# The end of a graph-attention layer issued together with the start of a top-p layer: shared banks and buffers, two hand-written first periods, graph parts loaded two ahead

## The chip, the cores and the metric

The kernel runs on one core of a Trainium2 chip. The metric is the device time of one execution in microseconds (us). Before the change three runs took 2077.24, 2079.14 and 2081.67 us; the median is 2079.14. The engines are named as in the profile: PE (matmul) and PEld (its weight loads), DVE (vector), ACT (scalar), POOL, and SP, whose queue (SPq) issues most transfers.

## What is computed

Two layers over N = 3327 nodes with 256 features and a dense 0/1 adjacency matrix. Both normalize and rectify their input and add their result to it.

```python
# layer 0: graph attention, 4 heads of 64
h = relu(layernorm(x))
support = (h @ weight) per head;  f1, f2 = support . weight_u, support . weight_v
attn = softmax over neighbours of leaky_relu(f1[m] + f2[n], 0.2)
x = x + attn @ support + bias + h @ proj_w.T + proj_b
# layer 1
h = relu(layernorm(x)); Xf = Xa = h; Z = 0
R = (adj + I) / row sums
for n in range(2):
    q = Xa @ W1.T @ W2.T;  k = Xa @ W3.T
    p = softmax(q @ k.T)
    A = p, only the largest entries of each row up to a sum of 0.9, normalized
    Xf = R @ Xf;  Xa = A @ Xa
    Z = Z + Xf @ U1[n].T + Xa @ U2[n].T
x = x + layernorm(h + Z) * ln_g + ln_b
```

## The kernel before

Rows are cut into NT = 26 tiles of 128 nodes (the last has 127).

**Layer 0** runs over four blocks of target nodes (tiles 0 to 5, 6 to 13, 14 to 21, 22 to 25). In each it goes over all 26 source tiles: a piece of the transposed adjacency is loaded (`load_adj`, L614), DVE makes one weight tile `w` per head (`weigh`, L581), and PE adds features and weight sums into PSUM (`sum_features` L590, `sum_weights` L601). POOL writes the adjacency back to DRAM as `adj_r` for layer 1. When a block is done, its sums are copied to `ot` (L675), and each of its row tiles passes through the class `Out` (L433): `divide` (transposes on PE), `normalize` (DVE, with three small POOL operations), `relu` (ACT, into `res`), `turn` (transposes on PE and a copy to `hT` on ACT), `keys` (the product with `wqk` on PE; `hi_and_lo` splits it in a high part on ACT and a low part on DVE), `take_keys` (two transfers into `k_sb`), `graph` (the product with `ug` on PE, two copies on ACT), `take_graph` (DVE), and stores on SP. For the first three blocks these steps are spread over the next block's steps. For the last block there is no next block: they stand alone, in L700 to L720, one row tile behind the other.

**Layer 1** runs two steps (s = 0 and 1). A step is a sequence of periods n. In each, a written list of words, a plan (`PLANS`, L1200), sets the order of work; each word names a role (`m2`, `m`, `a`, `b`, `c`, `d`: tile n+2, n+1, n, n-1, n-2, n-3) and a method of `Rows` (L798). A tile passes through

- `logits` 0 to 6 (L819): seven pieces of q times keys on PE. Piece 6 also needs the mean of all keys, which `mean_of_keys` puts behind the last key; `evict` (L831) copies a piece to `lg` by DVE (`v`) or ACT (`s`);
- `exp` (L839, ACT) and `guess` (L853, POOL): a first guess of where to cut the row;
- four times `probe` (L902): a pass of ACT over the row, which sums its exponentials behind the present guess; `go_on`, `aim` and `narrow` (ACT, DVE) make the next guess;
- `threshold`, `low` (L961), `largest` (L968), `last_kept`, `keep` (L1009): the exact cut, mostly on DVE;
- `transpose`, `copy_transposed`, `product` (L1019 to L1049): the kept row times the node features `xa`, on PE;
- small products and stores.

Beside this, R @ Xf is computed by `graph` (L737): per row tile seven parts of up to four chunks, each with a 256 KB load of `adj_r` (L748, three buffers `adjt`) and eight matmuls (L769, L770). The word `graph` in a plan issues the parts that are due: `PARTS` (L1283) gives the number for the first periods, and the rest of the 182 parts of a step are spread evenly over the other periods. `ends.dve` and `ends.act` finish a row of it (`add`, `high`, `low`).

The order on PE, DVE, ACT and POOL is the order of issue in the program (`in_traced_order`, L127); it isn't set for SP. Periods -3, -2 and -1 of step 0 hold the first words for tiles 0 and 1, after all of layer 0; the first plan serves n < 2. Layer 0's buffers (`p0`, `pa`, and the banks `ps1`) are given back before layer 1's (`px`, `pw`, `ps2`) are made; `lng`, `lnb` (L724) and `u_sb` (L1298) are loaded between them.

Of the kernel before, what the change touches and what calls it, by code (L numbers as in the profile page):

```python
# [10 lines left out]
FP = mybir.dt.float32  # L11
# [10 lines left out]
P = 128  # L22
# [32 lines left out]
def kernel(  # L55
# [189 lines left out]

    def part_of_keys(s, part):
        n = (EARLY if s else BLOCKS[-1][0] - 2) * P
        return ((0, n), (n, N))[part]
# [17 lines left out]
    def mean_of_keys(keys, s, part):  # L266

        k_sb, mean = keys
        n0, n1 = part_of_keys(s, part)
        nc.vector.tensor_reduce(  # L270
            mean[:, part : part + 1], k_sb[:, n0:n1].bitcast(FP), AX.X, ALU.add
        )
        if part == 1:
            nc.vector.tensor_scalar(
                k_sb[:, N:], mean[:, :1], mean[:, 1:], 1.0 / N, ALU.add, ALU.mult
            )

    EARLY = NT - 2

    def load_u(pool):  # L280
        u_sb = pool.tile([P, DC, 2, D], FP, name="u_sb")
        for n in range(STEPS):
            nc.sync.dma_start(out=u_sb[:, :, n, :], in_=u2t[n].rearrange("(c p) j -> p c j", p=P))
        return u_sb
# [23 lines left out]
    keys = new_keys(right)  # L308
    first_traced = len(nc.cur_bb.bb.instructions)
    with ExitStack() as l0:  # L310
        p0 = l0.enter_context(tc.tile_pool(name="p0", bufs=1))
        pa = l0.enter_context(tc.tile_pool(name="pa", bufs=2))
        ps = l0.enter_context(tc.tile_pool(name="ps1", bufs=1, space=PSUM))

        def bank(k, shape):
            return ps.tile(shape, FP, tag=f"b{k}", name="pt")

# [31 lines left out]
        sup = p0.tile([P, NT, D], FP, name="sup")  # L349
# [22 lines left out]
        def normalize(i):  # L372
            normed[i] = hn = pa.tile([P, D], FP, tag="x1", name="hn")
# [4 lines left out]
        def turn(i, k):  # L378
# [6 lines left out]
            hT = pa.tile([P, DC, P], FP, tag="hT", name="hT", bufs=4)  # L385
# [3 lines left out]
        def features(i, k):  # L389
# [9 lines left out]
            if i == t0:  # L399
                made["ef"] = pa.tile([H, 4, P], FP, tag="ef", name="ef", bufs=1)  # L400
            nc.scalar.activation(eas[:, i], f1, AF.Exp, scale=SLOPE)
            nc.scalar.activation(cf[:, i], f1, AF.Exp, scale=1.0 - SLOPE)
            nc.scalar.activation(made["ef"][:, i - t0], f2, AF.Exp, scale=SLOPE - 1.0)
            if i == t1 - 1:
                spread(t0, t1, made["ef"])
# [26 lines left out]

        class Out:  # L433
# [10 lines left out]
            def normalize(r):  # L444
# [5 lines left out]
                x1 = pa.tile([P, D], FP, tag="x1", name="x1")  # L450
# [33 lines left out]
            def turn(r, k):  # L484
# [6 lines left out]
                r.hT = pa.tile([P, DC, P], FP, tag="hT", name="hT", bufs=4)  # L491
# [56 lines left out]
        HP = H // 2  # L548
# [5 lines left out]
        for c in range(DC):  # L554
            for v, row in enumerate((u_row, v_row)):
                t = pa.tile([P, D], FP, tag="x1", name="wx")
# [14 lines left out]
        w1n = p0.tile([DA, DC, P], FP, name="w1n")  # L571
# [9 lines left out]
        def weigh(j, at, b, cn, *heads):  # L581
            pj = rows(j)
            for h in heads:
                ws[h] = w = pa.tile([P, CH], FP, tag="w", name="w", bufs=7)
# [29 lines left out]
        def load_adj(b, j):  # L614
            c0, pj = BLOCKS[b][0] * P, rows(j)
            cn = min(BLOCKS[b][1] * P, N) - c0
            ats[b, j] = at = pa.tile([P, CH], FP, tag="at", name="at", bufs=4)
# [11 lines left out]
        for step, (b, j) in enumerate(order):  # L629
# [41 lines left out]
            ot = pa.tile([P, HP + 1, CH], FP, tag="ot", name="ot", bufs=1)  # L671
# [28 lines left out]
        mean_of_keys(keys, 0, 0)  # L700
        n = len(outs)
        free = [3, 4, 5, 6, 7, 0, 1, 2]
        for k, r in enumerate(outs):
            r.divide(free[k])
        for k in range(n + 2):
            if k < n:
                outs[k].normalize()
            if 0 <= k - 2:
                outs[k - 2].keys(free[k - 2])
            if k < n:  # L710
                outs[k].relu()
            if 0 <= k - 2:
                outs[k - 2].take_keys()
            if 0 <= k - 1 < n:
                outs[k - 1].turn(free[n + k - 1])
        for k, r in enumerate(outs):
            r.graph(free[n + k])
            r.take_graph()
            r.store_keys()
            r.store()  # L720


    pl = ctx.enter_context(tc.tile_pool(name="pl", bufs=1))
    lng = row_of(pl, ln_g, "lng")  # L724
    lnb = row_of(pl, ln_b, "lnb")

# [10 lines left out]
    def graph(i, s, xf, ends):  # L737
# [5 lines left out]
        for g in range(NG):  # L743
            c0 = 4 * g
            a = pw.tile([P, 4, P], FR, tag="adjt", name="adjt", bufs=ADJ)
            cn = min(4, NT - c0)
            nf = min(cn, NF - c0)
            nc.sync.dma_start(  # L748
                out=a[:, :nf, :pn].bitcast(FP),
                in_=adj_r[c0 * P : (c0 + nf) * P, n0 : n0 + pn].rearrange("(c p) n -> p c n", p=P),  # L750
            )
            if nf < cn:
                move_rows(
                    nc.sync, a[:, nf, :pn].bitcast(FP), adj_r[NF * P :, n0 : n0 + pn], rows(NF)
                )
            if g == 3:
                while ends:
                    ends.pop(0)[1]()
                ad = pw.tile([P, D], FP, tag="ad", name="ad", bufs=1)
# [38 lines left out]
    class Rows:  # L798
# [32 lines left out]
        def evict(r, copy, *pieces):  # L831
            for p in pieces:
                if p == 0:
                    r.lg = pw.tile([P, N + 1], FP, tag="lg", name="lg", bufs=3)
# [4 lines left out]
        def exp(r):  # L839
# [8 lines left out]
            r.e = pw.tile([P, N], FP, tag="e", name="e", bufs=3)  # L848
# [53 lines left out]
        def probe(r):  # L902
# [3 lines left out]
            junk = pw.tile([P, N], F8, tag="junk", name="junk", bufs=1)  # L906
# [123 lines left out]
        def copy_transposed(r, copy, *groups):  # L1030
            for g in groups:
                pt = r.pt.pop(g)
                r.wt[g] = wt = pw.tile([P, 4, P], FP, tag="wt", name="wt", bufs=WT)
# [82 lines left out]
    def general_cut(i, s, k_sb, pows):  # L1116
# [42 lines left out]
        for m in range(MANT):  # L1159
# [42 lines left out]
            """  # L1202
            c.product.4 c.query ends.dve a.probe ends.dve m.logits.3 b.threshold m.logits.4
            c.product.3 ends.act m.evict.v.2 m.evict.s.4 m.evict.v.3 m.logits.5
            c.copy_transposed.v.5 a.go_on d.store_sum a.aim.1 d.high m.logits.6 c.product.5
            graph b.low a.probe c.transpose.1 graph m.evict.v.6 c.transpose.4
            c.copy_transposed.s.4 d.small_products c.product.2 m.evict.v.5 m.exp a.narrow.1
            m2.logits.0 graph c.transpose.2 c.product.0 a.aim.2 c.product.6 graph graph
            b.largest m2.logits.1 c.scale c.copy_transposed.v.2 a.probe d.store_features
            m2.evict.s.0 b.last_kept m2.logits.2 c.transpose.6 c.transpose.3 graph a.narrow.2  # L1210
            d.low_part b.keep c.copy_transposed.v.3 c.product.1 c.copy_transposed.v.0
            m2.evict.v.1 c.copy_features_t m.guess c.features_t a.aim.3 m3.queries a.probe
            c.transpose.0 a.narrow.3 c.copy_transposed.s.1 b.make_sure c.copy_transposed.v.6
            graph c.transpose.5
            """,
# [66 lines left out]

    PARTS = (  # L1283
        {-3: 0, -2: 0, -1: 3, 0: 7, 1: 8},
# [10 lines left out]
    with ExitStack() as fast:  # L1295
        ps = fast.enter_context(tc.tile_pool(name="ps2", bufs=2, space=PSUM))
        px = fast.enter_context(tc.tile_pool(name="px", bufs=1))
        u_sb = load_u(px)  # L1298
        pw = fast.enter_context(tc.tile_pool(name="pw", bufs=2))
# [9 lines left out]
        def parts_of_graph(s, xf):  # L1309
            for i in range(NT):  # L1310
                yield from graph(i, s, xf, graph_ends)
# [37 lines left out]

        for s in range(STEPS):  # L1350
            end = s == STEPS - 1
            plans = [[t.split(".") for t in p.split()] for p in PLANS[s]]
            for n in range(-3, NT + 3):
                plan = plans[0 if n < 2 else 1 if n < NT else 2]
                fills = sum(t == ["graph"] for t in plan)
                if s and n == -3:
                    continue
# [43 lines left out]
    with ExitStack() as gen:  # L1401
        ps = gen.enter_context(tc.tile_pool(name="ps3", bufs=2, space=PSUM))
# [101 lines left out]
```

## Time and profile before

| | us |
|---|---|
| median of three runs | 2079.14 |
| the profiled execution | 2080.33 |
| its span, first to last instruction | 2078.5 |
| layer 0 (to the last attention matmul) | 0 to 655.9 |
| from there to the first transpose of node tile 0 | 655.9 to 738.0 |
| steady periods of step s=0 | 25.98 each |
| steady periods of step s=1 | 23.8 to 24.0 each |

The span is shorter than the execution's own time by 1.8 us, which lie around it. Times below are us from the span's start. [...] The column of waits names what came last before an engine went on.

### The profile page before, as it was taken

The numbers are of one execution on the slowest core, as the hardware profiler recorded it, in microseconds if no ns is written. First come the engines' busy times: TensorE is split into PE (matmuls) and PEld (weight loads), VectorE is DVE, ScalarE is ACT, GpSimd is POOL, SyncE is SP. The second block draws the span as 40 slices with busy tenths as digits, with TensorE's granted clock in tenths as the row PEclk, the third lists the DMA queues.
The fourth block names the chain that finished last, engine by engine and source line by source line (L and its number), as shares of the span: only waits on it lengthen the run. The fifth ranks groups of instructions, "written<-read, shape, count | busy, mean of one in ns | idle before, by whom it ended". The sixth has DMA issues, their size and how long they took to land.

```text
span 2078.5 us, 34250 instructions
## 1 busy us (share of the span) xinstructions
PE 1988.8 (96%) x11474; PEld 1391.1 (67%) x11474; DVE 1710.0 (82%) x4055; ACT 1271.3 (61%) x1950; POOL 790.6 (38%) x1860
## 2 busy tenths in 40 slices
PE   7999999999998689999999999997999999999996
PEld 3343333233223578888888888876798898888885
DVE  5767888988886488888888888855899999999985
ACT  2110100101112788888888888838899999999982
POOL 3221231223332244444444444423554445544441
PEclk9999999999998899999999999999899999999998
DMA  5455556565564433333333333377244343344320
GB/s 180 140 163 175 196 191 226 168 217 191 171 190 138 136 86 101 102 96 99 103 98 103 102 100 103 102 220 206 64 105 117 104 108 95 101 106 111 99 74 20
DMA packets 318881, 270.60 MB, mean 130 GB/s; under 512 B 30200, under 2 KB 293879, under 8 KB 318568
## 3 DMA queue, kind: packets, MB, share of 16 engines
q1 hardware_dynamic: 304024, 216.04, 37.7%
q0 software_dynamic: 13504, 51.62, 7.0%
q8 instruction: 92, 1.51, 0.3%
q14 instruction: 93, 0.76, 0.1%
q10 hardware_dynamic: 1168, 0.67, 0.1%
HBM read 177.79 MB, written 88.62 MB: 128 GB/s over the span
## 4 chain that ended last, share of the span: by engine, by line
PE 49%; ACT 12%; DVE 3%; issue 2%; DMA 1%; POOL 0%; SPq 0%; ACTq 0%; DVEq 0%; POOLq 0%
PE acca L1046 23%; ACT junk L907 7%; PE pt L1025 6%; PE pg L826 6%; PE accr L769 5%; PE accr L770 5%; ACT e L849 2%; PE pz L1089 2%; DMA adjt<-adj_r 1%; ACT lg L837 1%; ACT aim L897 1%; DVE v L973 1%; ACT wt L1035 1%; PE pq L195 0%; PE pt L524 0%
## 5 line engine op out<-in xcount | busy, mean ns | idle before, releaser
L907 ACT ACTIVATE junk<-lg,at 128x3327 fp8e4<-128x3327 f32 (+1 forms) x208 | 637.8, 3067 | 13.0 <-POOL at L873 10.6
L588 DVE SCALAR_TENSOR_TENSOR w<-xf,cf,at 128x1024 f32<-128x1024 f32 (+4 forms) x416 | 425.6, 1078 | 52.3 <-PE pt L606 51.7
L769 PE MATMUL accr<-xf,adjt 128*128 128x258 f32 (+3 forms) x1352 | 367.8, 305 | 19.1 <-DMA adjt<-adj_r 15.3
L770 PE MATMUL accr<-xf,adjt 128*128 128x256 f32 (+1 forms) x1352 | 341.9, 285 | 0.0
L596 PE MATMUL pt<-w,sup 128*64 128x512 f32 (+5 forms) x1456 | 337.5, 576 | 1.1 <-DVE w L588 1.0
L1046 PE MATMUL acca<-xa,wt 128*128 128x256 f32 (+2 forms) x1352 | 317.9, 384 | 2.9 <-ACT wt L1035 2.9
L1046 PE MATMUL acca<-res,wt 128*128 128x256 f32 (+2 forms) x1352 | 317.8, 380 | 0.0
L769 PEld LDWEIGHTS accr<-xf,adjt 128*128 128x128 f32 (+1 forms) x1352 | 260.0, 192 | 29.5 <-DMA adjt<-adj_r 18.9
L1046 PEld LDWEIGHTS acca<-xa,wt 128*128 128x128 f32 (+2 forms) x1352 | 252.2, 192 | 36.0 <-ACT wt L1035 3.9
L1046 PEld LDWEIGHTS acca<-res,wt 128*128 128x128 f32 (+2 forms) x1352 | 247.7, 190 | 30.4 <-issue 0.7
L770 PEld LDWEIGHTS accr<-xf,adjt 128*128 128x128 f32 (+1 forms) x1352 | 260.8, 193 | 5.7
L826 PE MATMUL pg<-k_sb,q 128*128 128x512 f32 (+2 forms) x728 | 243.4, 427 | 15.4 <-DVE lg L837 6.7
L596 PEld LDWEIGHTS pt<-w,sup 128*64 128x64 f32 (+1 forms) x1456 | 95.2, 136 | 206.7 <-issue 136.8
L847 POOL TENSOR_SCALAR sc<-sc 128x1 f32<-128x1 f32 (+1 forms) x156 | 29.3, 216 | 510.1 <-ACT sc L845 510.1
L1025 PE MATMUL pt<-ident,e 128*128 128x128 f32 (+1 forms) x1352 | 194.5, 277 | 19.2 <-DVE e L1012 13.5
L973 DVE MAX8 v<-lg 128x8 f32<-128x416 f32 (+2 forms) x416 | 209.9, 577 | 0.1
L1025 PEld LDWEIGHTS pt<-ident,e 128*128 128x128 f32 (+1 forms) x1352 | 163.9, 145 | 60.1 <-ACT wt L1035 17.1
L964 DVE SCALAR_TENSOR_TENSOR lg<-e,th 128x3327 f32<-128x3327 f32 (+1 forms) x52 | 191.1, 3676 | 4.2 <-ACT th L957 4.2
L1012 DVE SCALAR_TENSOR_TENSOR e<-e,vm 128x3327 f32<-128x3327 f32 (+1 forms) x52 | 191.2, 3678 | 0.1
L1035 ACT COPY wt<-pt 128x512 f32<-128x512 f32 (+2 forms) x268 | 142.7, 545 | 57.9 <-PE pt L1025 41.2
L849 ACT ACTIVATE e<-lg,sc 128x3327 f32<-128x3327 f32 (+1 forms) x52 | 159.7, 3072 | 29.4 <-issue 26.9
L606 PE MATMUL pt<-w,eas 128*32 128x512 f32 (+5 forms) x1456 | 166.6, 568 | 0.0
(179 smaller groups left out, 2660.1 us busy)
## 6 DMA issues: line engine op xcount, KB each, us to landing
adjt<-adj_r SPq DMA_DIRECT2D x300, 256.0 KB, 3.1
at<-in_adj_t_dram SPq DMA_DIRECT2D x50, 512.0 KB, 5.9
adj_r<-at POOLq DMA_DIRECT2D x50, 512.0 KB, 5.3
at<-in_adj_t_dram SPq DMA_DIRECT2D x25, 384.0 KB, 3.2
adj_r<-at POOLq DMA_DIRECT2D x25, 384.0 KB, 3.5
qk_d<-qk SPq DMA_DIRECT2D x50, 128.0 KB, 2.2
q<-qk_d SPq DMA_DIRECT2D x100, 64.0 KB, 2.5
xf_d<-xf SPq DMA_DIRECT2D x50, 128.0 KB, 3.8
```

Source lines behind the costliest of these rows:

```text
L588: nc.vector.scalar_tensor_tensor(o, cb, cf[:pj, j, h : h + 1], a, ALU.max, ALU.mult)
L596: nc.tensor.matmul(acc[q * O : (q + 1) * O, :mn], sup[:pj, j, h * O : (h + 1) * O], ws[h][:pj, 512 * m : 512 * m + mn], start=(j == 0), st ...
L769: nc.tensor.matmul(acc[:pn, :dx], w, xc[:, :dx], start=begin, stop=False)
L770: nc.tensor.matmul(acc[:pn, :D], w, xc[:, DX:], start=False, stop=end)
L826: nc.tensor.matmul(r.pg[p][:pn, :mn], r.q[:, v, :pn], k_sb[:, m0 : m0 + mn], start=(v == 0), stop=(v == 1),)
L849: nc.scalar.activation(r.e[:pn], r.lg[:pn, :N], AF.Exp, bias=nmu[:pn], accum_out=r.ssum[:pn])
L907: nc.scalar.activation(junk[:pn], r.lg[:pn, :N], AF.Exp, bias=r.at[:pn, 4:], accum_out=r.g[:pn], saturate=False,)
L964: nc.vector.scalar_tensor_tensor(r.lg[:pn, :N], e, r.th[:pn], e, ALU.is_lt, ALU.mult, accum_out=r.below[:pn])
L973: nc.vector.max(r.v8[:pn, q], r.lg[:pn, q * w : min((q + 1) * w, N)])
L1012: nc.vector.scalar_tensor_tensor(e, e, r.vm[:pn, 1:], e, ALU.is_ge, ALU.mult, accum_out=kept[:pn])
L1025: nc.tensor.transpose(r.pt[g][: rows(c), j, : r.pn], r.e[: r.pn, c * P : c * P + rows(c)], ident[: r.pn, : r.pn],)
L1046: nc.tensor.matmul(r.acc[: r.pn], wt[: rows(c), j, : r.pn], xa[: rows(c), c, :], start=(c == 0), stop=(c == NT - 1),)
```

## The change

The bodies of most methods stay. What is changed:

1. **Shared memory.** One set of eight PSUM banks serves layer 0 and both steps; class `Banks` gives each name of layer 1 fixed banks in turn (`lg` three, `accr` two, `tr` two, `acca` one, as many as before). Buffers of layer 1 are views of tiles that layer 0 uses: two `lg` tiles hold six of the seven weight tiles and the two `x1` and `hn` tiles, `sup` holds two `e` tiles, and the four adjacency tiles of layer 0 hold `wt`, `junk`, `ad` and `u_sb`. The third `lg` and `e` come from `pw`, which is made after layer 0 is closed. `adjt` has a place of its own. `hT` has two buffers for layer 0's features and its first three blocks, before four; the four row tiles of the last block have one each.
2. **`end_of_layer_0`** takes the place of L700 to L720 and of periods -3 to -1 of step 0: it issues the last four row tiles of layer 0 and the logits, `exp` and `guess` of node tiles 0 and 1 mixed with each other, and three graph parts. Keys are summed in three pieces (tiles 0 to 19, 20 to 24, and 25) instead of two. `store` and `store_keys` of the four tiles come last.
3. **Two plans of their own** (`FILL`) for n = 0 and 1 of step 0. In n = 0 all logits, `exp` and `guess` of tile 2 are issued, and the graph gets 15 parts instead of 7; in n = 1 it gets 10 instead of 8. The 182 parts of the step stay the same in number.
4. **Graph parts are loaded two ahead** in both steps: at the place of part k the load of part k+2 is issued, across rows and across the two steps. The number of buffers stays three.
5. **`u_sb`** is loaded in n = 1 of step 0, **`lng` and `lnb`** in n = 1 of step 1.

```diff
+    KEY_PARTS = ((0, BLOCKS[-1][0] - 2, NT - 1, NT), (0, NT - 2, NT))
...
+    lgs = [right.tile([P, N + 1], FP, name=f"lg{k}") for k in range(2)]
+    sup = right.tile([P, NT, D], FP, name="sup")
+    both = sup.rearrange("p t d -> p (t d)")
+    at4 = right.tile([P, 4, WIDE * P], FP, name="at4")
+    flat = at4.rearrange("p k n -> p (k n)")
+    adjt = right.tile([P, 3, 4, P], FR, name="adjt")
+    slots = {
+        "lg": lgs + [None],
+        "e": [both[:, k * (N + 1) : k * (N + 1) + N] for k in range(2)] + [None],
+        "adjt": [adjt[:, k] for k in range(3)],
...
+    class Banks:
+        OF = {"lg": (0, 1, 2), "accr": (3, 4), "tr": (5, 6), "acca": (7,)}
...
+        weights = [t[:, k * WIDE * P : (k + 1) * WIDE * P] for t in lgs for k in range(3)]
+        weights.append(p0.tile([P, WIDE * P], FP, name="w"))
+        rows_of_adj = [at4[:, k] for k in range(4)]
...
-                r.hT = pa.tile([P, DC, P], FP, tag="hT", name="hT", bufs=4)
+                r.hT = hts[r.i - BLOCKS[-1][0] if r.i >= BLOCKS[-1][0] else r.i % 2]
...
+    def part_of_adj(s, i, g, ahead):
+        k = (s * NT + i) * NG + g
+        while len(loaded) <= min(k + ahead, STEPS * NT * NG - 1):
+            m = len(loaded)
+            loaded.append(load_part(m // NG % NT, m % NG))
+        return loaded[k]
...
+    FILL = (
+        """
+        graph a.probe a.go_on m2.logits.0 graph m2.logits.1 graph m2.evict.v.0 graph
+        m2.evict.v.1 m2.logits.2 graph a.aim.1 a.probe m2.logits.3 m2.evict.v.2 graph
+        ends.dve m2.evict.s.3 ends.act ends.dve m2.logits.4 m2.logits.5 a.narrow.1 graph
+        m2.evict.v.4 graph a.aim.2 a.probe graph m2.evict.s.5 m2.logits.6 a.narrow.2 graph
+        m2.evict.v.6 graph a.aim.3 a.probe graph m2.exp a.narrow.3 graph m2.guess
+        m3.queries graph ends.dve ends.act ends.dve
+        """,
+        """
+        b.threshold graph b.low a.probe a.go_on graph a.aim.1 graph a.probe graph b.largest
+        graph m2.logits.0 a.narrow.1 m2.evict.s.0 graph a.aim.2 a.probe m2.logits.1
+        b.last_kept graph b.keep m2.logits.2 m2.evict.s.1 graph a.narrow.2 b.make_sure
+        m3.queries graph ends.dve ends.act ends.dve a.aim.3 a.probe graph a.narrow.3
+        """,
+    )
     PARTS = (
-        {-3: 0, -2: 0, -1: 3, 0: 7, 1: 8},
+        {-3: 0, -2: 0, -1: 3, 0: 15, 1: 10},
         {-3: 0, -2: 0, -1: 6, 0: 10, 1: 7},
     )
...
+        def end_of_layer_0():
+            first, second = (new_tile(0, i) or tiles[0, i] for i in (0, 1))
+            part_of_adj(0, 0, 0, 2)
...
+            mean_of_keys(keys, 0, 0)
+            for k, r in enumerate(outs):
+                r.divide((5, 6, 7, 3)[k])
+            outs[0].normalize()
+            for p in range(3):
+                logits(first, p, "s")
+            outs[1].normalize()
+            outs[0].relu()
+            for p in (3, 4):
+                logits(first, p)
+            first.evict(copies["s"], 3)
+            outs[0].turn(4)
+            first.evict(copies["s"], 4)
+            outs[2].normalize()
+            outs[1].relu()
+            outs[0].keys(4)
+            outs[1].turn(5)
+            outs[3].normalize()
+            outs[0].take_keys()
+            logits(second, 0, "v")
+            for k in (2, 3):
+                outs[k].relu()
+                outs[k - 1].keys(3 + k)
+                outs[k].turn(4 + k)
+                outs[k - 1].take_keys()
+                logits(second, k - 1, "v")
+            outs[3].keys(7)
+            outs[3].take_keys()
+            outs[0].graph(4)
+            logits(first, 5, "s")
+            outs[1].graph(5)
+            for part in (1, 2):
+                mean_of_keys(keys, 0, part)
+            logits(first, 6, "v")
+            first.exp()
+            for k in (0, 1):
+                outs[k].take_graph()
+            first.guess()
+            logits(second, 3, "v")
+            outs[2].graph(6)
+            logits(second, 4, "s")
+            logits(second, 5, "v")
+            outs[3].graph(7)
+            logits(second, 6, "v")
+            second.exp()
...
+            filler(PARTS[0][-1])
+            second.guess()
+            for r in outs:
+                r.store_keys()
+                r.store()
+            new_tile(0, 2)
...
-            for n in range(-3, NT + 3):
+            for n in range(-2 if s else 0, NT + 3):
...
+                if not s and n < 2:
+                    plan = [t.split(".") for t in FILL[n].split()]
+                if not s and n == 1:
+                    u_sb = load_u(slots["u_sb"][0])
```

Here `logits(r, p, engine)` issues piece p of a tile's logits and, with an engine named, its eviction.

## The prediction

> **What bounds the kernel now.** I read the page's totals first, then busy time by stretch, then PE's waits in the worst stretch, then the timelines of PE, ACT, DVE and SP there.
>
> ```profile
> PE 1988.8 (96%) x11474; PEld 1391.1 (67%) x11474; DVE 1710.0 (82%) x4055; ACT 1271.3 (61%) x1950; POOL 790.6 (38%) x1860
> PEclk9999999999998899999999999999899999999998
> ```
>
> PE is busy 96% of the span, and its granted clock dips at the end of layer 0 (slices 13 and 14), between the two steps (s=0 and s=1) and at the end. By stretch (busy time of PE, PEld, DVE, ACT, POOL, then the granted clock, DMA share and GB/s):
>
> ```profile
> 655.90:738.00 82.10, 53.61 (x246) 40.46 (x242) 40.79 (x126) 51.03 (x72) 27.39 (x84) 0.81 0.45 125
> 738.00:767.70 29.70, 26.51 (x155) 23.08 (x155) 25.71 (x74) 23.31 (x37) 11.03 (x33) 0.94 0.28 71
> 767.70:1380.00 612.30, 609.33 (x3612) 531.70 (x3613) 529.07 (x1423) 522.69 (x784) 271.49 (x671) 0.99 0.40 108
> ```
>
> 655.9 is the end of layer 0's last attention matmul, 738.0 the first transpose of node tile 0 (period n=2). I call this stretch the ramp: PE is idle for 28.5 us of 82.1, and its clock averages 0.81. From 767.7 on PE is busy 609.3 of 612.3 us at full clock: there a period lasts what PE's work lasts. In the ramp nobody is full, so a chain of dependent work sets it. PE's waits in the ramp (total us, times, longest):
>
> ```profile
> PE pg L826 <- DVE lg L837: 6.1, 2, 5.4
> PE pt L498 <- ACT hT L492: 4.8, 4, 2.2
> PE accr L769 <- DMA ad<-p_d: 3.6, 1, 3.6
> PE pt L1025 <- DVE e L1012: 3.6, 1, 3.6
> PE accr L769 <- DMA adjt<-adj_r: 3.5, 6, 1.5
> ```
>
> The last link is the cut rows of tile 0 (L1012). Their chain, from the timelines: exponential, first of four probes, threshold, cut (`low`), keep (`keep`).
>
> ```profile
> 689.88 3.07 ACT L849 ACTIVATE e<-lg,sc 128x3327 f32<-128x3327 f32 x1 [0.45 <-DVE lg L837]
> ...
> 696.73 3.07 ACT L907 ACTIVATE junk<-lg,at 128x3327 fp8e4<-128x3327 f32 x1 [3.21 <-POOL at L873]
> ...
> 720.06 0.28 ACT L957 ACTIVATE th<-at,sc 128x1 f32<-128x1 f32 x1
> ```
>
> ```profile
> 721.00 3.68 DVE L964 SCALAR_TENSOR_TENSOR lg<-e,th 128x3327 f32<-128x3327 f32 x1
> ...
> 734.28 3.67 DVE L1012 SCALAR_TENSOR_TENSOR e<-e,vm 128x3327 f32<-128x3327 f32 x1
> ```
>
> The exponential starts only at 689.88, because no logits are issued before layer 0's last projection (L524) has ended at 681.65; meanwhile PE runs at half clock.
>
> **What the Trainium skill says.** "TensorE: Matmul & The Clock Gate", Part 1, says PE falls to half clock after about one idle window of 3.4 us and comes back after as long a busy one. The trace agrees: the granted clock is 0.50 in 660 to 670, and starts of L769 and L770 lie 0.21 us apart at 695 but 0.12 at 698. "Perfetto Trace Analysis", Identifying the Most-Contended Engine, warns that matmul busy time misleads because matmuls are pipelined. Here too: the page's mean for L769 is 305 ns, yet the next starts 0.12 us later, so I price by starts. "DMA: Bandwidth & Descriptors", Rules for kernel authors, says to issue a transfer early and wait late; the trace shows PE waiting 15.3 us in all for `adjt`.
>
> ```profile
> 697.60 0.28 PE L769 MATMUL accr<-xf,adjt 128*128 128x258 f32 x1
> 697.72 0.28 PE L770 MATMUL accr<-xf,adjt 128*128 128x256 f32 x1
> ...
> 698.55 1.92 PE L826 MATMUL pg<-k_sb,q 128*128 128x512 f32 x8
> ```
>
> **The change, part by part.** *Graph parts moved.* A part of four chunks takes 698.55 - 697.60 = 0.95 us; a row tile has 54 such matmuls in seven parts, so 54 x 0.12 / 7 = 0.93 us a part. Before, 3 + 7 + 8 = 18 parts lie ahead of n=2 and (182 - 18) / 24 = 6.83 in each of 24 periods; after, 3 + 15 + 10 = 28 lie ahead and 6.42 remain. A PE-bound period loses 0.42 x 0.93 = 0.386 us; 24 of them lose **9.3 us**. ACT and DVE need 22.2 and 22.5 us of a period (522.69 and 529.07 over 612.3/26 = 23.5 periods' worth), while the period goes from 25.98 (keeps start at 789.45 and 815.43) to 25.6. In step s=1 periods of 23.8 us (keeps at 1505.07 and 1528.89) run with these two engines 93% busy (448 and 449 of 480 us from 1520), so I count the saving whole; ends are 4 and 9.3.
>
> *The end of layer 0.* Logits 0 to 4 of tile 0 and 0 to 2 of tile 1 (0.47 us each at full clock) now fill PE's gaps from 657.8, before and between the turns. The queries they need are no wait: their loads were issued at 245.8 to 290, far ahead of use. `turn` follows each `relu` directly; the fourth tile's keys, before at 671.6 to 672.6 on PE, come at about 668.5, their copy to `k_sb` is issued near 670 (before at 673.27), and after the small means on DVE (0.94 us for 767 columns before) logit 6 goes at about 674.5. The exponential of tile 0 can then start near 676, against 689.88: 14 us earlier. Then ACT works through three exponentials and four probes (7 x 3.16 = 22.1), evictions and layer 0 copies (3 x 0.59 + 4 x 0.38 = 3.3), aims, `go_on` and two `high` (3.5) and three narrowings on DVE of about 1.3 us: 33 us, where before this piece took 30.2. Threshold at 709, 11 earlier. On DVE cut 3.7, maxima 4.0, a narrowing 1.5, `last_kept` 1.9, keep 3.7: 14.8 us, against 17.9 before, so n=2 begins near 724 rather than 738. Tile 1, whose last probe waits for `narrow.2` behind that keep, needs two more probes and follows with its threshold at about 734 against 744.83. So 11 us earlier on the slower of two paths. Every link here is an estimate from before's rows; I take **9 us**, ends -3 (a loss) and 13.
>
> *Work now inside the ramp.* Between about 682 and 724 PE must run 28 parts (26 us) and ten logits (4.7): 31 of 42 us at full clock, hidden; at half clock it would be 55 and show. Ten further loads of 256 KB go on SP. Before, it issued six in 9.14 us, held by buffers:
>
> ```profile
> 703.76 9.14 SPq L748 DMA_DIRECT2D adjt<-adj_r  x6
> ```
>
> That is 1.5 us a part; 25 parts then take 38 of the 42 us. Close, but beside the chain.
>
> *Loads two ahead.* A load moves two places up its queue and now waits there for the buffer of the part before; behind it on SP stand `ad`, stores and `q`, which have most of a period to spare. It can end PE's waits for `adjt`: 2.5 us in 800 to 1380 and 9.2 in 1380 to 1480. In the second stretch ACT is the chain (probe after probe from 1420.6), so most of the 9.2 becomes waiting for DVE's `e` (5.8 us there). I take 0, ends -1 (a loss) and 4.
>
> *Buffers, moved constant loads, no spare copies.* `lg`, `e`, `wt`, `junk` as views of shared tiles keep their counts (3, 3, 3, 1), and `hT` going from four to two still leaves each free before its second turn. Views of one tile don't serialize: DVE writes `sup` tiles while PE reads others, with PE full at 100 to 200 us. `u_sb` and the two rows leave the junction (SP 685.31 to 687.13) for quiet periods. Nothing, with 1 us either way.
>
> Sum: 9.3 + 9 = 18.3. The profiled execution took 2080.33 (span 2078.5 plus 1.8), so 2062.0; the median of runs, 2079.14, is 1.2 lower: **2061 us**.
>
> **Rivals.** *Only one of the two pays* (0.18): the ramp's chain slips by as much as it starts earlier, or ACT's chain holds the period at 26 us. For it: the sum on ACT grew by 3 us, and layer 0's copies now stand among its exponentials. Against: the shorter period of step s=1. Time 2079 - 9 = 2070. *More than that* (0.06): loads ahead and a warmer clock also shorten the second ramp by 4 and the first by 4 more: 2053. *No effect* (0.05): a new wait eats 15 us or more, 2079. *Slower* (0.17): the part loads pace the ramp. PE takes its queue in order, so tile 2's logits and tile 0's transposes stand behind 25 parts, each behind its load. With three buffers a round of three parts takes 4.5 us in the row above. The chain's 42 us allow 5 us a round; n=2 begins at before's 738 at 6.7, and the steady saving is eaten at 7.8 (8.3 rounds, 65 us from 682). At 9 us, with PE idle long enough in each round to fall to half clock, n=2 begins at 757: 19 late, less 9.3, gives 2089. For it: clock 0.81 and loads landing after up to 4.3 us; against: no round in before's trace is above 5.
>
> **How the numbers follow.** Forecast 0.54 at 2061, its own range 2054 to 2070: at the upper end half of the sum is lost, at the lower both uncertain ends come out well. With 2070, 2053 and 2079 that makes 0.83, so 2050 to 2082 leaves out the slower case. What a measurement can tell from no change is 0.2%, 4 us. Faster 0.54 + 0.18 + 0.06 = 0.78, same 0.05, slower 0.17.
>
> **What would show it.** Right: tile 0's exponential near 676, its keep ending near 724, `accr` waiting less than 2 us for `adjt` in the ramp, keeps 25.6 us apart. Wrong: keeps still 26 apart (no moved work paid), a first exponential after 685 (keys or means late), or PE idle behind `adjt` while ACT waits for `lg` (the slower rival). Attention itself should still end near 656; if not, the smaller `hT` set or the shared views cost there, which I put at nothing.

## The result, and the profile after

The changed kernel takes 2105.15 us (median of four, 2101.07 to 2110.8) against 2078.67 us for the kernel before on the same chip: a ratio of 1.0127, interval 1.0098 to 1.0157. It is 1.3% slower, where 0.9% faster was forecast; that is 23 us above the upper end of the predicted range (2082), and no rival names the place where the time went. The profiled execution (2101.07 us) is the fastest of the four: the traces account for 20.7 us of loss, and the other 6 us of the medians' difference were not seen in one.

The totals of the changed kernel's page, to be laid beside those of before:

```profile
PE 1991.1 (95%) x11474; PEld 1391.2 (66%) x11474; DVE 1706.7 (81%) x4053; ACT 1274.0 (61%) x1954; POOL 799.2 (38%) x1860
PEclk9999999999999999999999999999899999999998
```

The work on PE is the same to within 3 us, and the dip of the clock in slices 13 and 14 has gone. By these lines the change has worked. The page's row of PE in 40 slices gives a first sign of where it has not: slices 17 and 23 (840 to 892 and 1155 to 1207 us) have an 8 where the kernel before has a 9.

```profile
PE   7999999999999699899999899997899999999996
```

I split the span at two instructions that both kernels have: the keep (`keep`, DVE) of tile 0, the first that the pipeline waits for, and the keep of tile 25, the last of step s=0. All in us, of the profiled executions; the rows e1 to e9 are the experiments below.

| kernel | span | start to keep 0 | keep 0 to keep 25 | keep 25 to the end |
|---|---|---|---|---|
| before | 2078.5 | 734.28 | 640.7 | 703.5 |
| changed | 2099.2 | 724.80 | **670.8** | 703.6 |
| e1, share of before | 2065.2 | 717.51 | 644.1 | 703.6 |
| e2, end pieces at the row's end | 2066.3 | 723.90 | 639.7 | 702.7 |
| e3, 21 parts ahead | 2095.4 | 721.50 | **669.8** | 704.1 |
| e4, before with 28 parts ahead | 2120.9 | 744.67 | **670.1** | 706.1 |
| e5, e1 without loads ahead | 2066.6 | 718.86 | 642.7 | 705.0 |
| e6, e2 with tile 2's logits first | 2060.8 | 713.85 | 641.0 | 706.0 |
| e7, e1 with parts before stores | 2066.1 | 715.81 | 645.3 | 705.0 |
| e8, e1 with late end pieces | 2228.7 | 717.44 | **809.3** | 702.0 |
| e9, e1 with tile 2's logits first | 2066.7 | 717.17 | 645.2 | 704.4 |

Keep 0 starts 9.5 us earlier, nearly the 9 that the prediction took. Step s=1 did not change. All the loss, 30.1 us, lies in the 25 periods of step s=0, where 9.3 us were to be gained. It has two parts. From keep 0 to keep 2 the changed kernel takes 59.5 us, the one before 55.2; e1 and e2, which have no loss later on, take 59.7 and 59.1. So 4.3 us of the ramp's gain are given back there, and 5.1 are left at keep 2. The other 25.7 us are lost between keep 2 and keep 25. By stretch, the changed kernel (busy time of PE, PEld, DVE, ACT, POOL, then clock, DMA share, GB/s):

```profile
655.90:724.80 68.90, 55.28 (x303) 44.03 (x304) 35.37 (x120) 49.56 (x73) 29.57 (x95) 0.93 0.58 155
724.80:928.60 203.80, 183.09 (x1037) 158.81 (x1038) 157.99 (x434) 158.82 (x237) 73.73 (x185) 0.96 0.32 82
928.60:1082.00 153.40, 153.00 (x907) 132.56 (x906) 135.33 (x368) 136.43 (x204) 68.55 (x173) 1.00 0.38 98
1082.00:1252.00 170.00, 158.07 (x916) 137.44 (x915) 134.48 (x364) 136.71 (x203) 74.39 (x176) 0.97 0.34 87
1252.00:1380.00 128.00, 126.51 (x756) 109.68 (x754) 111.32 (x302) 110.16 (x166) 57.75 (x141) 1.00 0.39 100
```

The third line is what the prediction expected everywhere: six periods in 153.4 us, 25.57 us each, PE busy 99.7% of them. The fourth has six periods too, in 170.0 us: PE is idle for 11.9 us, and the mean clock is 0.97 instead of 1.00. The second, which also holds the end of the ramp, is of the same kind. Two blocks of disturbed periods with an undisturbed one between them: an average over the step would hide that. What PE waits for in the four disturbed periods from 784 to 880, and the longest wait of DVE there (us in total, times, longest):

```profile
DVE hl L833 <- ACT hl L830: 11.1, 4, 4.8
PE pt L1071 <- DVE e L1058: 6.5, 2, 4.5
...
PE pt L1071 <- DVE sup L1058: 4.6, 2, 4.2
```

PE's transposes (L1071) wait for the keep (L1058), at every one of the four keeps. The keep itself waits for nothing, but it stands behind `low` (L833) in the order of issue on DVE, and `low` waits for ACT's `high` (L830). The timelines of one such place (tile 4), first DVE, then ACT (start, duration; in brackets the idle time before and what ended it):

```profile
838.39 0.48 DVE L823 SCALAR_TENSOR_TENSOR at<-pt,rdeg,at 128x256 f32<-128x256 f32 x1
842.57 0.43 DVE L833 TENSOR_TENSOR hl<-at,hl 128x256 fp32r<-128x256 f32 x1 [3.70 <-ACT hl L830]
842.91 3.68 DVE L1058 SCALAR_TENSOR_TENSOR sup<-sup,vm 128x3327 f32<-128x3327 f32 x1
```

```profile
839.08 3.07 ACT L953 ACTIVATE at<-lg,at 128x3327 fp8e4<-128x3327 f32 x1
842.05 0.19 ACT L953 ACTIVATION_READ_ACCUMULATOR at<-lg,at 128x1 f32 x1
842.14 0.39 ACT L830 CAST hl<-at 128x256 fp32r<-128x256 f32 x1
```

`add` (L823) is done at 838.9, but ACT takes a probe (L953, 3.07 us) first, so `high` comes at 842.14, `low` at 842.57, and the keep at 842.91 instead of about 838.9. On PE (the same view):

```profile
846.75 1.94 PE L1071 MATMUL pt<-ident,sup 128*128 128x128 f32 x8 [4.17 <-DVE sup L1058]
```

So 4.2 us of PE are lost, and then more: the granted clock is 0.50 in 847 to 848 and 0.52 in 848 to 850. The Trainium skill says in "TensorE: Matmul & The Clock Gate", Part 1, on which the prediction drew for the ramp, that the clock falls to half after about one idle window of 3.4 us. This wait and the one at tile 5 (4.5 us) are longer than that, and the clock fell. But at tile 2 it fell after only 2.1 us (0.50 from 789), while a wait as long at tile 14 left it at 1.00. So how long PE must idle is not sharp in this trace, and it can be less than the page's window:

```profile
788.14 1.62 PE L1071 MATMUL pt<-ident,e 128*128 128x128 f32 x8 [2.09 <-DVE e L1058]
...
1114.10 1.06 PE L1071 MATMUL pt<-ident,e 128*128 128x128 f32 x8 [2.08 <-DVE e L1058]
```

```profile
789.00:790.00 1.00, 1.00 (x6) 0.90 (x5) 0.91 (x5) 1.00 (x2) 0.85 (x3) 0.50 0.01 3
1114.00:1116.00 2.00, 1.91 (x15) 1.73 (x16) 1.79 (x11) 1.24 (x2) 1.73 (x7) 1.00 0.41 115
```

Why do the end pieces stand there? The plan has words for them, `ends.dve`, `ends.act`, `ends.dve`, early in the period, far from the keep. But `graph` has a second rule, in both kernels: at a row's fourth part, where the one buffer `ad` is taken for this row, all end pieces of the row before that are still open are issued on the spot (L802 to L804; L756 to L758 before). Count the parts done at the end of a period, modulo the seven of a row. Before: 18 parts ahead and 6.83 a period give 3 for six periods and then less, so that a row's fourth part always comes in the period after the one in which the row before ended, behind the words. Changed: 28 ahead and 6.42 a period, so the place where a row ends slides through the whole period. Where it ends with the period's first, second or third part, the next row's fourth is the fifth, sixth or seventh part of the same period, and the pieces come out between the last graph words, right ahead of `m.guess b.keep`. By that count it happens in n = 3 to 6 and again, twelve periods later, in 15 to 18: the keeps of tiles 2 to 5 and 14 to 17. These are the disturbed blocks. Within a block the places differ. Where the row's fourth part comes with the fifth or sixth graph word (tiles 2, 3, 14 and 15), `low` waits 1.3 us. Where it comes with the last (tiles 4, 5, 16 and 17), `high` stands behind the plan's last probe on ACT, as in the timelines above, and `low` waits 3.7 to 4.8 us. The written period n = 1 has such a place too, ahead of keep 0: from tile 0's threshold to its keep it is 14.35 us here and 11.55 in e2, where no piece is forced there. How long DVE waited for `high` before `low`, over the whole run (us, times), first before, then changed:

```profile
  ACT hl L784: 1.2, 3
```

```profile
  ACT hl L830: 27.8, 12
```

This is theory F (forced end pieces); the expectations below name it and its rivals by letters.

### The profile page after: what moved, and what is told of

It reads as the page before. It is cut to its first block, busy times and chain, and to the rows that moved or that the text cites. A ratio compares the mean times of both kernels' runs of the same rounds, so it can differ in the third digit from the quotient of the medians.

```text
span 2099.2 us, 34320 instructions
## 1 busy us (share of the span) xinstructions
PE 1991.1 (95%) x11474; PEld 1391.2 (66%) x11474; DVE 1706.7 (81%) x4053; ACT 1274.0 (61%) x1954; POOL 799.2 (38%) x1860
## 4 chain that ended last, share of the span: by engine, by line
PE 75%; ACT 13%; DVE 5%; DMA 4%; issue 2%; POOL 1%; SPq 1%; ACTq 0%; DVEq 0%; POOLq 0%
PE pt L1092 21%; PE pt L655 15%; ACT at L953 8%; PE pt L665 8%; PE pt L1071 6%; PE pt L872 6%; PE pt L815 5%; PE pt L816 5%; PE pt L453 2%; DMA adjt<-adj_r 2%; PE pt L584 2%; PE pt L1135 2%; ACT sup L895 1%; ACT lg L883 1%; DVE sup L1058 1%
## 5 line engine op out<-in xcount | busy, mean ns | idle before, releaser
L953 ACT ACTIVATE at<-lg,at 128x3327 fp8e4<-128x3327 f32 (+1 forms) x208 | 637.8, 3066 | 11.9 <-POOL at L919 9.7
L647 DVE SCALAR_TENSOR_TENSOR lg<-xf,cf,at 128x1024 f32<-128x1024 f32 (+4 forms) x357 | 368.2, 1077 | 45.4 <-PE pt L665 45.1
L815 PE MATMUL pt<-xf,adjt 128*128 128x258 f32 (+3 forms) x1352 | 364.2, 303 | 23.1 <-DMA adjt<-adj_r 22.9
L816 PE MATMUL pt<-xf,adjt 128*128 128x256 f32 (+1 forms) x1352 | 339.2, 283 | 0.0
L655 PE MATMUL pt<-lg,sup 128*64 128x512 f32 (+3 forms) x1250 | 336.5, 576 | 1.1 <-DVE lg L647 1.0
L1092 PE MATMUL pt<-res,at 128*128 128x256 f32 (+2 forms) x1352 | 319.6, 382 | 1.0 <-ACT at L1081 1.0
L1092 PE MATMUL pt<-xa,at 128*128 128x256 f32 (+2 forms) x1352 | 317.0, 383 | 2.8 <-ACT at L1081 2.8
L815 PEld LDWEIGHTS pt<-xf,adjt 128*128 128x128 f32 (+1 forms) x1352 | 257.9, 191 | 35.2 <-DMA adjt<-adj_r 24.4
L1092 PEld LDWEIGHTS pt<-xa,at 128*128 128x128 f32 (+2 forms) x1352 | 251.9, 192 | 35.7 <-ACT at L1081 3.8
L1092 PEld LDWEIGHTS pt<-res,at 128*128 128x128 f32 (+2 forms) x1352 | 249.9, 192 | 32.6 <-ACT at L1081 1.8
L816 PEld LDWEIGHTS pt<-xf,adjt 128*128 128x128 f32 (+1 forms) x1352 | 258.7, 191 | 5.2
L1071 PE MATMUL pt<-ident,sup 128*128 128x128 f32 (+2 forms) x910 | 131.9, 278 | 21.7 <-DVE sup L1058 12.1
L1071 PEld LDWEIGHTS pt<-ident,sup 128*128 128x128 f32 (+2 forms) x910 | 110.1, 145 | 50.6 <-ACT at L1081 17.3
```

Of the source, the lines that this page charges most:

```text
L647: nc.vector.scalar_tensor_tensor(o, cb, cf[:pj, j, h : h + 1], a, ALU.max, ALU.mult)
L655: nc.tensor.matmul(acc[q * O : (q + 1) * O, :mn], sup[:pj, j, h * O : (h + 1) * O], ws[h][:pj, 512 * m : 512 * m + mn], start=(j == 0), st ...
L815: nc.tensor.matmul(acc[:pn, :dx], w, xc[:, :dx], start=begin, stop=False)
L816: nc.tensor.matmul(acc[:pn, :D], w, xc[:, DX:], start=False, stop=end)
L953: nc.scalar.activation(junk[:pn], r.lg[:pn, :N], AF.Exp, bias=r.at[:pn, 4:], accum_out=r.g[:pn], saturate=False,)
L1071: nc.tensor.transpose(r.pt[g][: rows(c), j, : r.pn], r.e[: r.pn, c * P : c * P + rows(c)], ident[: r.pn, : r.pn],)
```

## The experiments

Ratios are to the kernel before, run beside each on the same chip; the intervals are 95%.

**e1: the share of before.** One line of the changed kernel; everything else of the change stays.

```diff
-        {-3: 0, -2: 0, -1: 3, 0: 15, 1: 10},
+        {-3: 0, -2: 0, -1: 3, 0: 7, 1: 8},
```

> The changed kernel with the graph's parts shared as before (3, 7, 8, then 6.83 a period). Theory F (the new share lets a graph row end early in a period, so that the next row's fourth part forces the three end pieces of it, add, high and low, right ahead of keep on DVE, and DVE waits there for ACT): no such period is left from n=2 on, keeps lie 26 us apart throughout, DVE waits before the low piece for under 3 us instead of 27.8, the gain of the first periods stays, 2066 to 2074. Rival V (shared views and loads two ahead make waits of their own in the steady periods): periods of 28 to 32 us stay, 2095 or more.

Measured 2068.0 us (2066.67 to 2069.98), ratio 0.9947 (0.993 to 0.9964). The ten parts that the change moved forward cost the kernel 37 us in all. There is no disturbed block: keeps are 25.9 us apart on the mean from 803 to 1295. DVE's wait in `low` in this run:

```profile
  ACT hl L830: 2.3, 3
```

Shared banks, views, two loads ahead and the joint order are all still in this kernel, so none of them is the cause by itself.

**e2: the end pieces at the row's own end.** The changed kernel with its 28 parts, a second `ad`, and the forced issue moved from the fourth part to the seventh, just before the row's own pieces are queued. They now come out at their words, or at the latest with the next row's last part.

```diff
-        "ad": [flat[:, 28 * P : 28 * P + D]],
+        "ad": [flat[:, k * P : k * P + D] for k in (28, 30)],
...
             if g == 3:
-                while ends:
-                    ends.pop(0)[1]()
                 ad = buffer("ad", [P, D], FP, 1)
...
+        while ends:
+            ends.pop(0)[1]()
         ends.append(("dve", add))
```

> The changed kernel with two ad buffers, and the end pieces forced only at the next row's seventh part, so that they come where the plan's words put them. All 28 parts still lie ahead of n=2. Theory F: keeps 25.6 us apart, DVE's wait before the low piece under 3 us, 2057 to 2067, faster than both kernels. Rival V: 2095 or more. Rival G (the moved parts are to blame by overloading the first periods): 2080 to 2100, with the loss ahead of n=4.

Measured 2071.89 us (2068.05 to 2072.24), ratio 0.9963 (0.9948 to 0.9977). The 31 us of step s=0 are back (639.7 against 670.8) with the share unchanged. So it is the place of the pieces and not the share itself. DVE's wait in `low` is above the 3 us that were expected, but 3.7 of it lie before 731 us, in the two written periods:

```profile
  ACT hl L828: 4.2, 4
```

But the time is 5 us above the top of what was expected. Against e1, keep 0 comes 6.4 us later and the step is only 4.4 us shorter: moving ten parts ahead pays nothing even without the forced pieces.

**e3 and e4: other shares, the other kernel.** e3 is the changed kernel with `0: 10, 1: 8` (21 parts ahead), e4 the kernel *before* with `0: 15, 1: 10` as its only edit. One run each.

> The changed kernel with 3, 10 and 8 parts ahead of n=2, seven fewer than in the change and three more than before, 6.71 a period. Theory F: the row's end then falls early in nine periods in a row, n=3 to 11 (keeps of tiles 2 to 10), which last 27 to 32 us, while all later ones last 25.7 to 26; in all 2090 to 2110. Rivals V and G: between the change and the old share, without such a block of nine; G below 2085.

> The kernel before with only the numbers of parts changed to 3, 15 and 10. Theory F: the same two blocks of four long periods (keeps of tiles 2 to 5 and 14 to 17) as in the change, DVE's wait before the low piece 20 to 30 us, 2095 to 2115. Rival V: no long periods, since nothing is shared or loaded ahead here, 2068 to 2080.

e3 took 2097.27 us. The count for 21 parts and 6.71 a period gives one block, n = 3 to 11, and keeps of tiles 2 to 10 come 30.6, 27.3, 26.5, 27.3, 27.3, 27.3, 32.2, 32.1 and 33.1 us apart, then 25.4 to 26.0 up to tile 22. Most of the 30.6 belongs to the ramp (29.9 in e1). Of the others, those of tiles 3 to 7 have the fourth part with the fifth or sixth graph word and those of tiles 8 to 10 with the last: 26.5 to 27.3 us and 32.1 to 33.1, the two kinds of place again. e4 took 2123.01 us, and has the two blocks of the changed kernel without anything else of the change. DVE's wait in `low` in e4:

```profile
  ACT hl L784: 27.1, 12
```

Theory F holds in both, with the places given by the count. e4 lies 8 us above its upper bound; its keep 0 also comes 10 us later (744.67 against 734.28), which the bound had not allowed for.

**e5: no loads ahead.** e1 with `graph(i, s, xf, graph_ends, 0)` in place of 2.

> As e1_old_share (parts shared as before), but each part loaded at its own place again. Theory P (loading two ahead is worth nothing on the path, as the prediction put it, -1 to 4 us): within 4 us of e1, 2064 to 2072, with PE waiting for adjt 5 to 12 us longer in all. Rival P2 (it carries part of e1's gain): 2073 or more, keep of tile 0 after 722.

Measured 2067.74 us (2066.64 to 2068.42), ratio 0.9946 (0.993 to 0.9963), which is e1's time. PE waits for `adjt` 17.7 us in the whole run, against 16.9 in e1. 5 to 12 us more were expected. With this share the loads two ahead do nothing that can be seen; with 28 parts ahead they were not tried.

**e6: tile 2's logits first.** e2 with the first period's plan reordered. In e2 ACT waits 5.8 us for logits of tile 2 that stand in PE's queue behind graph parts, which wait for their loads. Here four pieces of logits go ahead of the parts, and the end words behind the third probe.

```diff
-        graph a.probe a.go_on m2.logits.0 graph m2.logits.1 graph m2.evict.v.0 graph
-        m2.evict.v.1 m2.logits.2 graph a.aim.1 a.probe m2.logits.3 m2.evict.v.2 graph
...
+        m2.logits.0 m2.logits.1 a.probe a.go_on m2.logits.2 m2.evict.v.0 m2.evict.v.1
+        m2.logits.3 m2.evict.v.2 graph graph a.aim.1 a.probe m2.logits.4 m2.evict.s.3
...
```

> As e2_ends_at_words (28 parts ahead, ends at the plan's words), with the same words of the first written period in another order: tile 2's logits 0 to 3 stand ahead of the graph parts, and the end pieces behind the third probe. Theory Q (keep of tile 0 comes 6 us later in e2 than in e1 because PE's queue holds tile 2's logits behind parts that wait for loads, and ACT's queue waits for their eviction ahead of its next aim): ACT's longest wait before an eviction falls from over 5 us to under 2, keep of tile 0 at 717 to 720 instead of 723.9, in all 2064 to 2069. Rival Q2 (ten more parts simply take PE's time): keep of tile 0 at 722 or later, 2070 or more.

Measured 2069.05 us (2062.61 to 2069.84), ratio 0.9956 (0.9939 to 0.9972). Keep 0 starts at 713.85, 10 us before e2's. Part of that lies ahead of the ramp: layer 0 ended earlier in this execution, and tile 0's first logits were copied at 656.24, against 659.46 in e2. From that copy to keep 0 it is 57.6 us instead of 64.4, and the 6.8 us come from where theory Q looks for them. In e2 tile 0's second and third probe start 12.3 us apart (688.06 and 700.38), with this copy between them on ACT:

```profile
696.96 0.59 ACT L883 COPY lg<-pt 128x512 f32<-128x512 f32 x1 [5.76 <-PE pt L872]
```

In e6 they start 5.2 us apart (684.50 and 689.70), and the copy between them waits for nothing. The same two probes are 12.2 us apart in the changed kernel, which also has 15 parts in that period, 10.7 in e3 with 10 and 7.1 in e1 with 7. The list of ACT's waits in 655 to 740 still has one of 6.5 us for logits, where under 2 us was expected:

```profile
ACT lg L883 <- PE pt L872: 8.4, 2, 6.5
```

But those 6.5 us end at 716.55, after keep 0 has started, so they do not delay it. Keep 1 follows 31.7 us after keep 0, in e2 30.8, and the medians of e2 and e6 can't be told apart; the profiled execution is the fastest of e6's four by 6.4 us. That the order of the logits helps the whole is not shown. The end words were moved along with the logits; which of the two did how much was not tried.

**e7: the parts before the stores.** In e1 the fourth part, the first of period n = 0, waits 4.3 us for its load, which stands on SP behind layer 0's stores. Here `filler(3)`, the first three parts with the loads two ahead, is issued before `take_graph` of the last two row tiles, which stores.

```diff
+            filler(PARTS[0][-1])
             for k in (2, 3):
                 outs[k].take_graph()
-            filler(PARTS[0][-1])
```

> As e1_old_share, with the first three graph parts issued ahead of the last two row tiles' take_graph, so that their loads stand ahead of those stores on SP. Theory S (PE's wait of 4.3 to 5 us for the fourth part comes from 22 stores ahead of its load on SP): that wait falls to 2 us or less, keep of tile 0 1 to 3 us earlier, 2064 to 2067. Rival: the load then stands at the head of SP waiting for its buffer and holds the stores; no change, 2066 to 2070.

Measured 2067.86 us (2067.36 to 2069.3), ratio 0.995 (0.9933 to 0.9967). PE in 655 to 740:

```profile
PE pt L1071 <- DVE sup L1058: 10.5, 1, 10.5
PE pt L1071 <- ACT at L1081: 3.9, 1, 3.9
PE pt L815 <- DMA adjt<-adj_r: 3.2, 5, 0.9
PE pt L815 <- POOL at L932: 3.1, 1, 3.1
```

By this list the wait for `adjt` fell from 8.1 us to 3.2. But 3.1 us before the fourth part are now put down to POOL (L932), though that matmul reads only `xf` and `adjt`; it starts at 685.43 instead of 686.56, so its wait fell from 4.3 us to 3.1 and not to 2 or less. Keep 0 moved 1.7 us forward. Half of this is given back at once: keep 1 comes 30.7 us after keep 0, where e1 has 29.8. At keep 25 0.4 us are left, and the time is the same.

**e8: the suspected cost, in every period.** e1, in which nothing slides, with the three end words taken from their early places in the steady plan of s=0 and put behind its last graph word. No part moves.

```diff
-            graph c.copy_features_t c.query a.probe graph m.guess b.keep a.narrow.3
+            graph c.copy_features_t c.query a.probe graph ends.dve ends.act ends.dve m.guess b.keep
+            a.narrow.3
```

> After with the share of before (18 parts ahead, so nothing drifts), and the row's end pieces of step s=0 put by the plan itself right behind the period's last graph word, ahead of the guess and the keep, in every steady period, instead of at their early words. No part is moved and nothing is added. Theory F (the end pieces ahead of the keep are what costs; some 31 us over eight periods in the changed kernel, so 3.9 a period): keeps of step s=0 29 to 31 us apart nearly throughout, DVE's wait in low for ACT's high in most of 24 rows (40 to 100 us in all), and 70 to 130 us on the whole: 2138 to 2200. Rival (the loss of the changed kernel came from how many parts a period holds, and the forced pieces only went with it): 2068 give or take 4, keeps 26 apart.

Measured 2230.53 us (one run): 162 us more than e1, all of it between keep 0 and keep 25. Keeps are 31.7 to 35.5 us apart up to tile 24. The rival is out. The time lies 30 us above the top of what F gave: in e8 rows end late in the period, so `add` waits for PE's last part as well. DVE before L822, the first instruction of `add`, and before `low`:

```profile
  PE pt L816: 58.4, 18
```

```profile
  ACT hl L830: 51.7, 26
```

**e9: the logits first, with the share of before.** e1 with the first period's plan of e6.

> After with the share of before (18 parts ahead) and, in the first period's plan, tile 2's logits ahead of the graph parts and the end words behind the third probe, as in the run with the logits first. Theory Q (PE's queue holds the logits behind parts that wait for loads): tile 0's keep starts at 706 to 714 against 717.5 with the same share in the old order, and some of it stays: 2060 to 2066. Rival (tile 1's chain sets the end of this stretch, as where the loads were put ahead of the stores): the keep comes earlier, the gap to tile 1's keep grows by as much, and the whole stays at 2066 to 2070.

Measured 2065.94 us (2063.32 to 2068.55), ratio 0.9933 (0.992 to 0.9947). Keep 0 starts at 717.17, in e1 at 717.51. From the first logits copy to keep 0 it is 57.3 us against 58.5, and keep 1 gives 0.8 us of that back (30.6 us later, in e1 29.8). So with 18 parts ahead the order of the logits gains little there, much as the rival has it. e9 has the lowest median, but its runs overlap those of e1, e5 and e7, so it is not shown to be better than they are. All of these beat both kernels; the simplest is e1, one line away from the changed kernel.

## Why the prediction was wrong

- **The step that failed** is the one headed *Graph parts moved*: "A PE-bound period loses 0.42 x 0.93 = 0.386 us; 24 of them lose **9.3 us**", and "so I count the saving whole". In its place step s=0 became 30.1 us longer, 25.7 of it after keep 2. The step priced the parts by PE's time and asked whether DVE and ACT were too busy. They were not. It did not ask where in the period the row's *other* pieces (`add`, `high`, `low`) come out once 6.42 parts instead of 6.83 make a period. They are tied to part numbers and not to the plan, and the step had taken the plan's words for their place. Between keep 2 and keep 25 this costs 30.6 us (611.3 in the changed kernel, 580.6 in e2). e2 (same share, pieces freed: the 31 us return), e4 (share alone, in the kernel before: the two blocks appear) and e8 (pieces late, nothing moved: 162 us) show this from three sides.
- **The sum.** 18.3 us of gain were forecast and the profiled span grew by 20.7, 39 us apart. The forced pieces after keep 2 are 30.6 of them; the saving of the moved parts came to 4.9 us instead of 9.3 (585.5 us before, 580.6 in e2); and the ramp gained 5.1 us by keep 2 instead of 9.
- **The size of the loss** can be read from the second block: its six periods take 170.1 us, 16.7 more than six undisturbed ones. PE's idle time of 11.9 us is the larger part of this; I put the rest down to the clock of 0.97, 0.03 x 170 = 5 us. This division is worked out, not measured by itself.
- **Even free of that, the saving was over-sized.** 0.386 us a period were predicted. From keep 2 to keep 23 e2 takes 538.9 us, e1 543.4 and the kernel before 544.0: 0.22 to 0.24 us a period. The prediction started from 25.98, which is a period with seven parts; over the twelve periods from keep 2 the mean is 25.93 before, 25.82 in e1 and 25.73 in e2. The shorter periods take 25.0 in e1, and 25.0 to 25.7 in e2. Where these tenths go is open.
- **"Work now inside the ramp" was not hidden.** It was counted as nothing. From tile 0's first logits copy to keep 0 it is 58.5 us in e1 with 18 parts and 64.4 in e2 with 28: 6 us. That outweighs the 4.4 us saved in the step. 5.2 of the 6 lie between tile 0's second and third probe (7.1 us in e1, 12.3 in e2): ACT has to copy a piece of tile 2's logits there first, and on PE that piece stands behind more graph parts and their loads. e6 takes it away by its order. PE waits 11.2 us for `adjt` in the ramp of the changed kernel, nine times, where under 2 was expected; the longest wait, 5.0 us, is for the fourth part, whose load stands behind stores on SP.
- **The end of layer 0 was right up to the threshold.** In the changed kernel (ACT):

```profile
673.76 3.07 ACT L895 ACTIVATE sup<-lg,sc 128x3327 f32<-128x3327 f32 x1
...
710.45 0.29 ACT L1003 ACTIVATE th<-at,sc 128x1 f32<-128x1 f32 x1
```

  The exponential was predicted near 676, the threshold at 709, and the end of tile 0's keep near 724; it ended at 724.80 + 3.68 = 728.5, against 738.0 before. 2.8 us of the 4.5 that it is late are the forced pieces ahead of keep 0. That the sum gives the threshold is in part luck: the exponential came 2 us earlier than predicted, and the wait between the second and third probe, which the sum doesn't have, used that up and 1.5 us more. With the share of before (e1) the ramp gains 16.8 us to keep 0 and 12.3 to keep 2, above the 9 taken. e1's gain over the kernel before, 11.6 us by the medians, comes from here.
- **Loads two ahead, buffers and views** were put at nothing. e5 shows it for the loads, with the share of before. Shared tiles and views were not tried by themselves, but e1 has them all, and its step s=1 and its undisturbed periods are those of before.
- **The rivals.** The slower one had a time in the neighbourhood (2089), which is luck: it put the loss in the ramp, which got shorter. Its mechanism is there in small, tile 2's logits behind parts and their loads, and so is the sign named for it (PE waits 11.2 us for `adjt`, ACT 9.2 us for `lg`), but by e1 and e2 it cost 6 us, where the rival had n=2 begin 19 us late. That "only one of the two pays" is near to what e1 and e2 show, 2068 and 2072, but it, too, supposed that the moved parts cost nothing where they don't pay.

## What to carry to other kernels

When a change alters how many pieces of a side task go into a period, follow the task's *boundaries* through all the periods, not only its load: a single buffer that is handed over at a fixed piece drags its release along, and where the rate no longer divides the period it drags it past every point of the plan, the worst one too. What it is dragged behind matters too: ahead of the last probe a forced row cost some 1.3 us of period, behind it 6 to 7 (e3). Read periods one by one (the start of one instruction that each has) before taking a mean: here about half of the 25 took what was predicted, and two blocks of some six cost it all. And an engine that is busy 99% of a stretch is no promise that work taken from it comes back in full (4.9 us of 9.3 here), nor that the place it is moved to is free (6 us more in the ramp).

## What was unexpected of the hardware

A wait can cost about half as much again as its length, as the granted clock falls behind it (the periods of e3 with waits of 4.5 us are 6 to 7 us longer than the others): after 4.17 us without a matmul PE ran at 0.50 to 0.52 from 847 to 850, and in e8, with such a wait in nearly every period, the mean clock from 803 to 1297 was 0.92, against 1.00 in e1. The clock was at half after every wait for a keep of 3.6 us or more between 745 and 1400 us in these traces, after none of 1.2 us or less, and at 2.1 us after some and not after others (0.50 behind tile 2's keep in the changed kernel, 1.00 behind tile 14's).
